# Layer 1 as seven half-size products, q read in PSUM, and sums kept in idle gather rows

## The chip, the cores and the metric

The kernel runs on one core of a Trainium2 chip. The metric is device time in microseconds (us) of one execution; lower is better. All data is 32-bit floating point, and a TensorE product in that type is recorded as two passes.

## The reference

x is (32, 512, 1024): 32 batches, each a matrix of 512 rows (channels) by 1024 columns (nodes). adj is 512 x 512. For every batch:

```python
q, k = wq . x, wk . x                         # 1024 numbers each
scores = leaky_relu(q[None, :] + k[:, None])  # slope 0.01
att = softmax(scores, axis=-1)                # 1024 x 1024
agg = einsum('cn,mn->cm', x, att)
x = layernorm(x + relu(adj @ agg + bm))       # layer 0
W = adj * adj                                 # support and kernel are both adj
x = layernorm(x + W^T @ x + bias)             # layer 1
```

## The kernel before, in words

Layer 0 never forms the 1024 x 1024 attention. Since adj is applied linearly, the kernel first projects x (`project`, L213): for each of 8 column tiles z it makes zrow, a row per node with q, the 512 projected channels and k. With the nodes sorted by q, each softmax row is a combination of a prefix sum and a suffix sum of these rows. So per batch:

- `spread` (L233) puts q along the free axis on all partitions: eight TensorE transposes into a PSUM tile qb, copied to an SBUF tile qs (L241).
- `place` (L256, VectorE) compares qs with the q of one node tile and sums up to that tile's ranks; `send` (L268, GpSimd) scatters the rows of zrow to DRAM in rank order. `count` (L292, ScalarE) counts with a Sign how many q lie above -k, and `top` (L286) takes the largest q.
- `fetch` (L317) brings the sorted rows back to SBUF (zs) in nine blocks, `weigh` (L334) makes the weight matrices lw, and `table` (L356) makes the prefix and suffix sums: nine steps, one after the other. A step is a TensorE product into PSUM tile tp, a ScalarE copy to ts (L368), and two small copies of the carry row into zs for the next step: one on GpSimd (L372), one on ScalarE (L374). The table goes to DRAM.
- `share` (L300) makes the indices, `pick` (L381, GpSimd) gathers from the table into g, eight tiles of three rows' length each (own row, two sums). `shares`, `scale` and `gain` mix the three into u, in place: a ScalarE product (L432) and two VectorE operations (L440) per tile.
- `turn` (L474) transposes u into PSUM and applies the Relu on ScalarE to give y; `join` (L485) adds x and takes the statistics on VectorE; `root` (L454) makes the reciprocal root on GpSimd (L457, L458); `shift` (L461) and `apply` (L467, ScalarE) finish the normalization. Each batch has four row blocks of 128 channels (0 to 3).

Layer 1 (`layer1`, L494) multiplies y by w1, which is adj * adj plus the identity, so that the residual is part of the product. A batch takes 4 x 2 output tiles of 128x512, each a sum of 4 products: 32 products. `stats1` (L515) adds the bias while reading PSUM, and takes the statistics of v.

The batches overlap, three or four at a time. The order on each engine is written out by hand (`tc.manual_schedule()`); each engine runs its own queue strictly in the order of the program, and the build puts semaphore waits where data or buffers require them. `slot(s)` (L659) is one step of the pipeline, for s from 1 to 29:

- TensorE projects batch new = s + 2 tile by tile (z from 0 to 7); in the later half it also runs the table steps of mid = s + 1 and the turns of batch s, and old = s - 1 is normalized and stored.
- then come the spread of new, the last table step of mid and layer 1 of s, with place, count, send, pick and fetch issued among the products.

`begin`, `opening` and `end` fill and drain the pipeline. PSUM has two pools: `ps_mm` with three tiles of two banks for projections, turns, spread and layer 1, and `ps_t` with one for the table steps.

Of the kernel before, what the change touches and what calls it, by code (L numbers as in the profile page):

```python
# [8 lines left out]
F32 = mybir.dt.float32  # L9
# [14 lines left out]
def gat_gcn_resnorm_kernel(  # L24
# [37 lines left out]

    nc = tc.nc
# [19 lines left out]
    gpool = ctx.enter_context(tc.tile_pool(name="gpool", bufs=1))  # L83
# [107 lines left out]

    w1 = adj_sb
    nc.vector.tensor_tensor(w1, adj_sb, adj_sb, ALU.mult)
    for ct in range(CT):
        nc.vector.tensor_tensor(
            w1[:, ct, ct * P : (ct + 1) * P], w1[:, ct, ct * P : (ct + 1) * P], ident, ALU.add
        )

# [5 lines left out]
    gs = {}  # L204
# [28 lines left out]
    def spread(b, copy=nc.scalar.copy):  # L233

        qb = ps_mm.tile([P, N], F32, name=f"qb_{b}", tag="mm")
        for nt in range(NT):
            nc.tensor.transpose(  # L237
                qb[:, nt * P : (nt + 1) * P], zrow[:, nt, 0:1].to_broadcast([P, P]), ident
            )
        qs = junk.tile([P, N], F32, name=f"qs_{b}", tag="qs")  # L240
        copy(qs, qb)  # L241
# [114 lines left out]
    def table(b, step, by=nc.gpsimd):  # L356

        lt, td = tabs[b][0], tds[b].rearrange("(s w u) c -> s w u c", w=2, u=3)
        tp = ps_t.tile([P, 2, H], F32, name=f"tp_{b}_{step}", tag="t")
# [21 lines left out]
    def pick(b, mt):  # L381

        idx = info[b][0]
        if mt == 0:
            gs[b] = gpool.tile([P, NT, 3 * ZW], F32, name=f"g_{b}", tag="g")
        nc.gpsimd.indirect_dma_start(  # L386
            out=gs[b][:, mt, :],
# [7 lines left out]
    def own(b, k0=0, k1=NT):  # L395

        idx, ac, kc, tl = info[b]
        if k0 == 0:
            g = gs.pop(b).rearrange("p k (u c) -> p k u c", u=3)
            ra = small.tile([P, NT, 3], F32, name=f"ra_{b}", tag="ra")  # L400
            mixes[b] = (g, ra)
# [92 lines left out]
    def layer1(b, mt, h, cts=range(CT), op=None):  # L494

        yt = ys[b]
        if op is not None:
            ops[b, mt] = op
        elif (b, mt) not in ops:
            ops[b, mt] = ps_mm.tile([P, N], F32, name=f"o1_{b}_{mt}", tag="mm")  # L500
        for ct in cts:
            nc.tensor.matmul(  # L502
                ops[b, mt][:, h * H : (h + 1) * H],
                w1[:, ct, mt * P : (mt + 1) * P],
                yt[ct][:, h * H : (h + 1) * H],
                start=(ct == 0),
                stop=(ct == CT - 1),
            )

    def layer1g(b, mts, ct):  # L510
        for mt in mts:
            for h in range(NH):
                layer1(b, mt, h, (ct,))

    def stats1(b, mt):  # L515
        t = vpool.tile([P, N], F32, name=f"v_{b}_{mt}", tag="v")
        nc.vector.tensor_tensor(t, ops.pop((b, mt)), bias_bc, ALU.add)  # L517
        stats((1, b, mt), t)
        vs[b, mt] = t
# [4 lines left out]
    def last(b, mt):  # L524

        t = vpool.tile([P, N], F32, name=f"v_{b}_{mt}", tag="v")
        st = small.tile([P, NH, 6], F32, name=f"st_1_{b}_{mt}", tag="st")
        mv = small.tile([P, 2], F32, name=f"mv_1_{b}_{mt}", tag="mv")
        halves = [slice(h * H, (h + 1) * H) for h in range(NH)]
        ops_last = (  # L530
            ps_t.tile([P, N], F32, name="last_0", tag="t"),
            ps_mm.tile([P, N], F32, name="last_1", tag="mm"),
        )
        for h in range(NH):
            layer1(b, mt, h, op=ops_last[h])
        for h, some in enumerate(halves):
            op = ops_last[h]
            nc.vector.tensor_tensor(t[:, some], op[:, some], bias_bc[:, some], ALU.add)
            nc.vector.bn_stats(st[:, h, :], t[:, some])
            if h == 0:  # L540
                shift(1, b, mt - 1)
                apply(1, b, mt - 1)
                store(b, mt - 1)
        nc.vector.bn_aggr(mv, st)
        due[1, b, mt] = [t, mv]
        root(1, b, mt)
        shift(1, b, mt)
        t, mv, rs, nb = due.pop((1, b, mt))
        nc.scalar.activation(t[:, halves[0]], t[:, halves[0]], AF.Identity, bias=nb, scale=rs)
        nc.vector.tensor_scalar(  # L550
            t[:, halves[1]], t[:, halves[1]], rs, nb, ALU.mult, ALU.add
        )
        for some in halves:
            nc.sync.dma_start(out=out[b, mt * P : (mt + 1) * P, some], in_=t[:, some])

    def begin():
# [5 lines left out]
        spread(0)  # L562
# [16 lines left out]
        spread(1)  # L579
        for z in range(NT):  # L580
# [14 lines left out]
            if z == NT // 2 - 1:  # L595
                for mt in range(NT // 2):
                    pick(0, mt)
# [7 lines left out]
            if z == NT - 3:  # L605
                table(1, 0)
                for mt in range(NT // 2, NT):
# [5 lines left out]
        spread(2)  # L613

    def opening():

        shares(0, 0, NT // 2)
        for k in range(NT // 2):
            scale(0, [k])
            gain(0, [k])  # L620
            if k % 2:
                table(1, 3 + k // 2)
        share(1)
        shares(0, NT // 2, NT)
        for k in range(NT // 2, NT):
            scale(0, [k])
            gain(0, [k])
            if k % 2:
                table(1, 3 + k // 2)
# [9 lines left out]
        for mt in range(NT):  # L639
            pick(1, mt)  # L640
        for nt in range(NT):
            order(2, nt)
            count(2, nt)
        top(2)
        fetch(2)
        for ct in range(CT):
            layer1g(0, range(CT - 1), ct)
# [203 lines left out]
```

## Time and profile before

| what | us |
|---|---|
| median of 3 runs (2403.43 to 2408.95) | 2404.76 |
| the profiled execution, its own time | 2408.18 |
| its span, from first to last instruction | 2406.5 |
| TensorE busy (PE) | 2304.5 |
| VectorE busy (DVE) | 1671.5 |
| ScalarE busy (ACT) | 1440.2 |
| GpSimd busy (POOL) | 1019.1 |

The mean granted TensorE clock was 0.98 of full speed. In the profile, PE is TensorE's matmul and PEld its weight load, DVE is VectorE, ACT ScalarE, POOL GpSimd and SP the queue that issues most transfers. L502 means line 502 of the kernel. A group's line reads: line, engine, operation, output<-inputs, shape, count, then busy time and the mean duration of one in ns, then the idle time of the engine just before and what ended it. A line of a timeline reads: start, duration, engine, line, operation, and in brackets the idle time before it. Matmuls are pipelined, so a group's mean duration is longer than the distance from start to start.

### The profile page before, as it was taken

Reading aid. Unit: us, or ns where it says so; the run is one execution under the profiler, and the core shown is the slowest. Engines: PE = TensorE matmul, PEld = TensorE weight load, DVE = VectorE, ACT = ScalarE, POOL = GpSimd, SP = SyncE. Lnnn points to the kernel's source line nnn. Section 1 sums busy time; section 2 is a strip of 40 time slices with the busy share of each in tenths; the row PEclk is TensorE's granted clock in tenths of the full one; section 3 lists DMA queues with packets and bytes.
Section 4 is the critical chain, followed back from the end, with each engine's and each line's share of the span. In section 5 each row is a group of like instructions: output and inputs, shape, how many; then the busy total and the mean of one; then the engine's idle time right before and its main releaser. Section 6 shows DMA issues by size and latency. Waiting matters only on the chain.

```text
span 2406.5 us, 30937 instructions
## 1 busy us (share of the span) xinstructions
PE 2304.5 (96%) x9744; PEld 1450.5 (60%) x9744; DVE 1671.5 (69%) x3485; ACT 1440.2 (60%) x2213; POOL 1019.1 (42%) x1289
## 2 busy tenths in 40 slices
PE   8778999999999999999999999999999999999876
PEld 7545665666665666656566666566666556666433
DVE  3266777767777676777776777767677777677745
ACT  2465656765665775655676655667565566666642
POOL 1333444434444433444533444543444453344431
PEclk9988999999999999999999999999999999999987
DMA  6556777667776767776767777676777676777651
GB/s 241 166 182 219 252 237 250 215 222 250 250 254 230 234 208 241 256 250 231 249 206 232 248 259 242 234 233 212 244 254 253 229 246 206 235 248 252 204 198 48
DMA packets 176836, 548.68 MB, mean 228 GB/s; under 512 B 26304, under 2 KB 26304, under 8 KB 176672
## 3 DMA queue, kind: packets, MB, share of 16 engines
q1 hardware_dynamic: 117600, 276.65, 39.1%
q0 software_dynamic: 57344, 269.52, 29.5%
q8 instruction: 78, 1.28, 0.2%
q14 instruction: 86, 0.70, 0.1%
q10 hardware_dynamic: 1728, 0.53, 0.1%
HBM read 338.17 MB, written 208.43 MB: 227 GB/s over the span
## 4 chain that ended last, share of the span: by engine, by line
PE 78%; DMA 5%; DVE 5%; ACT 4%; issue 4%; POOL 4%; SPq 0%; POOLq 0%; ACTq 0%; DVEq 0%
PE zp L221 32%; PE o L502 30%; PE tp L363 11%; PE op L478 3%; DVE g L440 3%; DMA g<-td,idx 3%; POOL zs L372 2%; ACT y L482 1%; PE qb L237 1%; ACT w L344 1%; DMA zs<-td 1%; ACT ts L368 1%; DVE st L449 1%; DMA td<-zrow,ranki 1%; POOL td L271 1%
## 5 line engine op out<-in xcount | busy, mean ns | idle before, releaser
L221 PE MATMUL zp<-wmT,x 128*128 128x257 f32 x4096 | 968.3, 388 | 3.0 <-ACT zrow L229 3.0
L502 PE MATMUL o<-y,adj_sb 128*128 128x512 f32 x2032 | 891.1, 596 | 6.5 <-ACT y L470 3.6
L221 PEld LDWEIGHTS zp<-wmT,x 128*128 128x128 f32 x4096 | 764.3, 191 | 202.1 <-issue 92.5
L502 PEld LDWEIGHTS o<-y,adj_sb 128*128 128x128 f32 x2032 | 382.1, 191 | 478.6 <-issue 464.2
L372 POOL COPY zs<-ts 1x513 f32<-1x513 f32 x254 | 203.1, 800 | 671.8 <-ACT ts L368 671.8
L440 DVE SCALAR_TENSOR_TENSOR g<-g,ra 128x512 f32<-128x512 f32 x512 | 370.5, 750 | 36.7 <-ACT g L432 27.6
L271 POOL DMA_INDIRECT td<-zrow,ranki x256 | 283.1, 1106 | 194.7 <-DVE ranki L266 124.9
L363 PE MATMUL tp<-zs,lw 128*64 128x257 f32 x2304 | 324.1, 400 | 40.4 <-POOL zs L372 29.7
L229 ACT COPY zrow<-zp 128x514 f32<-128x514 f32 x256 | 148.7, 581 | 327.4 <-PE zp L221 314.5
L262 DVE SCALAR_TENSOR_TENSOR lt<-qs,zrow,first 128x1024 int8<-128x1024 f32 x256 | 326.8, 1277 | 3.7 <-ACT qs L241 2.2
L386 POOL DMA_INDIRECT g<-td,idx x256 | 267.1, 1043 | 89.2 <-issue 78.9
L296 ACT ACTIVATE sg<-qs,kc 128x1024 int8<-128x1024 f32 x256 | 294.1, 1149 | 7.0
L489 DVE TENSOR_TENSOR y<-y,x 128x1024 f32<-128x1024 f32 x128 | 156.8, 1225 | 155.8 <-ACT y L482 154.1
L363 PEld LDWEIGHTS tp<-zs,lw 128*64 128x64 f32 x2304 | 149.4, 138 | 182.6 <-POOL zs L372 70.6
L457 POOL TENSOR_SCALAR rs<-mv 128x1 f32<-128x1 f32 x256 | 78.7, 307 | 400.5 <-ACT v L470 295.0
L368 ACT COPY ts<-tp 128x514 f32<-128x514 f32 x288 | 168.7, 586 | 109.9 <-PE tp L363 106.6
L408 ACT ACTIVATE ac<-s 128x4 f32<-128x4 f32 x64 | 13.3, 208 | 331.6 <-DVE s L407 331.6
L432 ACT ACTIVATE g<-g,ra 128x512 f32<-128x512 f32 x256 | 167.4, 713 | 57.8 <-DVE ra L419 57.7
L458 POOL TENSOR_TENSOR rs<-rs,mhalf 128x1 f32<-128x1 f32 x256 | 186.5, 728 | 21.3
L464 DVE SCALAR_TENSOR_TENSOR nb<-mv,rs 128x1 f32<-128x1 f32 x256 | 39.9, 159 | 217.9 <-POOL rs L458 217.9
L517 DVE TENSOR_TENSOR v<-o,bias_bc 128x1024 f32<-128x1024 f32 x127 | 154.6, 1218 | 31.7 <-PE o L502 31.5
L470 ACT ACTIVATE v<-v,nb,rs 128x1024 f32<-128x1024 f32 x126 | 154.8, 1231 | 33.0 <-DVE nb L464 33.0
(77 smaller groups left out, 1623.7 us busy)
## 6 DMA issues: line engine op xcount, KB each, us to landing
x<-in_x_dram SPq DMA_DIRECT2D x128, 512.0 KB, 3.7
out_dram<-v SPq DMA_DIRECT2D x127, 512.0 KB, 5.5
td<-ts SPq DMA_DIRECT2D x512, 120.5 KB, 2.2
zs<-td SPq DMA_DIRECT2D x64, 602.3 KB, 6.9
zs<-td SPq DMA_DIRECT2D x64, 240.9 KB, 3.5
zs<-td SPq DMA_DIRECT2D x96, 120.5 KB, 3.5
td<-ts SPq DMA_DIRECT2D x64, 96.4 KB, 2.9
td<-zs SPq DMA_DIRECT2D x8, 514.0 KB, 9.5
```

Of the source, the lines that this page charges most:

```text
L221: nc.tensor.matmul(zp[:, h, 0:CE], xb[ct][:, nt * P : (nt + 1) * P], wmT[:, ct, h * CE : (h + 1) * CE], start=(ct == 0), stop=(ct == CT - 1),)
L262: nc.vector.scalar_tensor_tensor(lt, qs, zrow[:, nt, 0:1], first[:, o : o + N], ALU.subtract, ALU.is_lt, accum_out=rank[:, nt : nt + 1],)
L271: sc = nc.gpsimd.indirect_dma_start(out=td[:, :], out_offset=bass.IndirectOffsetOnAxis(ap=ranki[:, nt : nt + 1], axis=0), in_=zrow[:, nt, ...
L296: nc.scalar.activation(sg, qs, AF.Sign, bias=kc[:, nt : nt + 1], accum_out=sgn[:, nt : nt + 1])
L363: nc.tensor.matmul(tp[i * G : (i + 1) * G, h, 0:CE], lt[:, i, j, :], zs[:, j, h * CE : (h + 1) * CE], start=True, stop=True,)
L368: nc.scalar.copy(ts.rearrange("p (h c) -> p h c", h=2), tp[:, :, 0:CE])
L372: by.tensor_copy(zs[0:1, to, 1:ZW], ts[0:1, 1:ZW])
L386: nc.gpsimd.indirect_dma_start(out=gs[b][:, mt, :], out_offset=None, in_=tds[b].rearrange("(s u) c -> s (u c)", u=3), in_offset=bass.Indir ...
L432: nc.scalar.activation(u, u, AF.Copy, scale=ra[:, k, 1:2])
L440: nc.vector.scalar_tensor_tensor(u, g[:, k, i, 1 : C + 1], ra[:, k, i : i + 1], u, ALU.mult, ALU.add)
L458: nc.gpsimd.tensor_tensor(rs, rs, mhalf, ALU.pow)
L502: nc.tensor.matmul(ops[b, mt][:, h * H : (h + 1) * H], w1[:, ct, mt * P : (mt + 1) * P], yt[ct][:, h * H : (h + 1) * H], start=(ct == 0), ...
```

## The change

1. `layer1` splits w1 and y into quarters (256 channels by 256, and 256 by 512) and forms seven products of quarters in place of eight, after Strassen's scheme in Winograd's form. It needs four sums of w1's quarters, S1 to S4, made once, and four sums of y's quarters per batch, T1 to T4. A product is two output tiles of 128x512, each a sum of two: 28 products of 128x512 a batch. The results lie in a PSUM tile per product; `read` adds them into v on VectorE, 18 operations of 128x512 a batch.
2. `sums` makes T1 on VectorE and T2 to T4 on GpSimd, into parts of the gather tile (now one constant tile, `rows`) whose rows 5 to 7 are not yet gathered for the next batch; pick 5, 6 and 7 wait until the products have read them.
3. In the slots `spread` leaves q in PSUM (in `ps_t`), and place, count and top read it there.
4. The slot is ordered anew: turns and joins run from z = 4 in place of 3, the old batch's v is normalized in pairs (0 and 1 on VectorE, 2 and 3 on ScalarE), and `phase` holds the new order of spread, layer 1 and exchange.

```diff
+    lo, hi = slice(0, H), slice(H, N)
+    nc.vector.tensor_tensor(bias_bc[:, hi], bias_bc[:, hi], bias_bc[:, lo], ALU.subtract)
...
+    rows = const.tile([P, NT, 3 * ZW], F32, name="rows")
+    room = {
+        ("T1", 0): (5, 2), ("T2", 0): (5, 0), ("T2", 1): (5, 1),
+        ("T1", 1): (6, 0), ("T3", 1): (6, 2), ("T3", 0): (6, 1),
+        ("T4", 0): (7, 0), ("T4", 1): (7, 2),
+    }
...
-    def spread(b, copy=nc.scalar.copy):
-        qb = ps_mm.tile([P, N], F32, name=f"qb_{b}", tag="mm")
+    def spread(b, copy=False):
+        pool, tag = (ps_mm, "mm") if copy else (ps_t, "t")
+        qs = pool.tile([P, N], F32, name=f"qb_{b}", tag=tag)
...
-        qs = junk.tile([P, N], F32, name=f"qs_{b}", tag="qs")
-        copy(qs, qb)
+        if copy:
+            qb, qs = qs, vpool.tile([P, N], F32, name=f"qs_{b}", tag="v")
+            nc.scalar.copy(qs, qb)
...
+    def sums(b, *some):
...
+            of, less = {
+                "T1": (y1[:, hi], y1[:, lo]), "T2": (y2[:, hi], t1),
+                "T3": (y2[:, hi], y1[:, hi]), "T4": (y2[:, lo], t2),
+            }[name]
+            (nc.vector if name == "T1" else nc.gpsimd).tensor_tensor(t, of, less, ALU.subtract)
...
+        for w, y in (
+            ("A11", "Y11"), ("S1", "T1"), ("S2", "T2"), ("S3", "T3"),
+            ("S4", "Y22"), ("A22", "T4"), ("A12", "Y21"),
+        ):
+            for m in range(2):
+                mul.append(lambda w=w, y=y, m=m: make(w, y, m))
+        for m in range(2):
+            u, v = m, 2 + m
+            for name, what in (
+                ("c1", (u, lo, "A11", m)),
+                ("c5", (v, hi, "S1", m)),
+                ("u2", (u, hi, "S2", m, u, lo)),
+                ("u3", (v, lo, "S3", m, u, hi)),
+                ("u4", (u, hi, None, m, v, hi)),
+                ("12", (u, hi, "S4", m, u, hi)),
+                ("22", (v, hi, None, m, v, lo)),
+                ("21", (v, lo, "A22", m, v, lo)),
+                ("11", (u, lo, "A12", m, u, lo)),
+            ):
...
+    def phase(s, mid, new, step=None):
+        mul, get, reads = layer1(s)
+        def rank(*some):
+            for nt in some:
+                if step is not None:
+                    place(new, nt)
+                    count(new, nt)
+                if nt < 3:
+                    send(new, nt)
+        if step is not None:
+            table(mid, step, pool=ps_mm)
+        mul[0]()
+        mul[1]()
+        sums(s, ("T2", 1), ("T3", 1), ("T4", 1))
+        rank(0, 1, 2)
+        mul[2]()
+        mul[3]()
+        get["c1", 0]()
+        rank(3)
+        get["c1", 1]()
+        rank(4, 5)
+        for mt in range(5):
+            pick(mid, mt)
+        reads("c5")
+        mul[4]()
+        mul[5]()
+        pick(mid, 5)
+        rank(6)
+        get["u2", 0]()
+        rank(7)
+        get["u2", 1]()
+        send(new, 3)
+        send(new, 4)
+        mul[6]()
+        mul[7]()
+        pick(mid, 6)
+        for nt in range(5, NT):
+            send(new, nt)
+        reads("u3", "u4")
+        mul[8]()
+        mul[9]()
+        reads("12", "22")
+        mul[10]()
+        mul[11]()
+        pick(mid, 7)
+        fetch(new)
+        reads("21")
+        mul[12]()
+        mul[13]()
+        shares(mid, 0, NT // 2)
+        scale(mid, range(NT // 2))
+        reads("11")
+        gain(mid, range(NT // 2))
+        if step is not None:
+            top(new)
...
     def slot(s):
...
         for z in range(NT):
-            step, ot = 2 * (z - tz), z - oz
+            step, ot = 2 * (z - tz), z - tz
+            if z == NT - 1:
+                turn(s, CT - 1)
+                sums(s, ("T1", 0), ("T1", 1))
+                join(s, CT - 1)
+                root(0, s, CT - 1)
+                sums(s, ("T2", 0), ("T3", 0), ("T4", 0))
             project(new, z, 0)
...
             if step >= 0:
-                table(mid, step + 1)
+                table(mid, step + 1, pool=ps_mm if z == NT - 1 else ps_t)
...
+            if ot == 2:
+                for mt in (2, 3):
+                    shift(1, old, mt)
+                    apply(1, old, mt)
+                    store(old, mt)
...
-        spread(new, nc.vector.tensor_copy)
-        layer1(s, 0, 0, range(0, CT // 2))
-        table(mid, NB - 1)
...
+        spread(new)
+        shift(0, s, CT - 1)
+        apply(0, s, CT - 1)
+        phase(s, mid, new, NB - 1)
```

## The prediction

> **What bounds the kernel now.** The page first: TensorE is busy almost all the time, and the two costliest groups are its own.
>
> ```profile
> span 2406.5 us, 30937 instructions
> PE 2304.5 (96%) x9744; PEld 1450.5 (60%) x9744; DVE 1671.5 (69%) x3485; ACT 1440.2 (60%) x2213; POOL 1019.1 (42%) x1289
> L502 PE MATMUL o<-y,adj_sb 128*128 128x512 f32 x2032 | 891.1, 596 | 6.5 <-ACT y L470 3.6
> ```
>
> Layer 1 (L502) is 891 us. Next, TensorE's timeline of one slot, from the spread of q (L237):
>
> ```profile
> 1030.16 1.09 PE L237 MATMUL qb<-ident,zrow 128*128 128x128 f32 x8
> 1031.09 1.88 PE L502 MATMUL o<-y,adj_sb 128*128 128x512 f32 x4
> 1032.90 1.09 PE L363 MATMUL tp<-zs,lw 128*64 128x257 f32 x8
> 1033.92 26.02 PE L502 MATMUL o<-y,adj_sb 128*128 128x512 f32 x60
> 1059.77 14.08 PE L221 MATMUL zp<-wmT,x 128*128 128x257 f32 x64
> ```
>
> The columns are start and duration. A pass of 128x512 costs (1059.77 - 1033.92)/60 = 0.431 us. The spreads of slots 1 and 29 start at 246.92 and 2241.55, so a slot takes 71.24 us, some 0.3 of it idle. The 29 slots are most of the span. So what counts is whether TensorE stays fed; which waits would end last is read from the other engines' timelines. VectorE (place) and ScalarE (count) work on one q at the same time:
>
> ```profile
> 1034.03 1.28 DVE L262 SCALAR_TENSOR_TENSOR lt<-qs,zrow,first 128x1024 int8<-128x1024 f32 x1
> 1035.42 1.27 DVE L262 SCALAR_TENSOR_TENSOR lt<-qs,zrow,first 128x1024 int8<-128x1024 f32 x1
> 1034.52 1.15 ACT L296 ACTIVATE sg<-qs,kc 128x1024 int8<-128x1024 f32 x1
> 1035.79 1.15 ACT L296 ACTIVATE sg<-qs,kc 128x1024 int8<-128x1024 f32 x1
> ```
>
> A place every 1.39 us and a count every 1.27, side by side. The tail of a row block goes from engine to engine:
>
> ```profile
> 1095.87 1.11 ACT L482 ACTIVATE y<-op,bm_sb 128x1024 f32<-128x1024 f32 x1 [0.28 <-PE op L478]
> 1097.01 1.23 DVE L489 TENSOR_TENSOR y<-y,x 128x1024 f32<-128x1024 f32 x1 [1.66 <-ACT y L482]
> 1098.27 1.29 DVE L449 BATCH_NORM_STATS2 st<-y 128x6 f32<-128x512 f32 x2
> 1099.59 0.21 DVE L451 BATCH_NORM_AGGREGATE mv<-st 128x2 f32<-128x12 f32 x1
> 1100.54 0.60 POOL L372 COPY zs<-ts 1x513 f32<-1x513 f32 x1 [1.84 <-ACT ts L368]
> 1101.13 0.21 POOL L457 TENSOR_SCALAR rs<-mv 128x1 f32<-128x1 f32 x1
> 1101.42 0.57 POOL L458 TENSOR_TENSOR rs<-rs,mhalf 128x1 f32<-128x1 f32 x1
> ```
>
> Here GpSimd's carry copy (L372), which the next table step on TensorE needs, stands ahead of the root (L457, L458) of the last row block: nothing on TensorE waits for that root at once.
>
> **The change, part by part.** Below, every time is in us, U is the start of the last table step ahead of the spread (step 7), and order and waits are those of the built programs.
>
> *Removed from TensorE.* 56 passes for 64: 8 x 0.431 = 3.45 a slot, on the path. That leaves 71.24 - 0.3 - 3.45 = 67.5 of TensorE work. The three layer-1 passes outside the slots save 10 more; I let sums and waits there eat that, net 0 (between -10 and +20).
>
> *Reads and sums on VectorE.* Out go four additions of 128x1024 (1.22, pitch 1.26) and the copy of qb (1.23); in come 18 of 128x512 (0.69 by L538, pitch 0.72: 13.0), two T1 (1.4) and two applies moved from ScalarE (0.81 each by L472): +10.6, VectorE 51.9 to about 62 of a slot. That fits only while it seldom waits.
>
> *q read in PSUM.* In the changed program each place waits for the count before it on ScalarE, and each count for its place; before, there is no such wait. Place 1.28, handing over 0.05, count 1.25 with its accumulator read, 0.05: 2.63 a pair. The first count also stands behind the copy of table step 8. (A count from PSUM is not in the trace; ScalarE's copy of qb took 1.01 and its Sign from SBUF 1.15, so 0 to 1.1 less in all.) Queued behind these waits on VectorE are the reads that free PSUM for TensorE. VectorE's queue from U: first count ends 5.6, place 3 ends 12.1, both c1 12.9, place 5 17.4, both c5 18.9, place 7 22.9, second u2 23.6, ten reads to 30.8, shares 1.55 to 32.4, two reads to 33.8, eight gain operations of 0.74 to 39.7, top 1.4 to 41.1, shares 42.7, a wait for scale 0.8, eight more gains 49.4, first weights (lw) 49.9. TensorE without waits would stand at the first table step at U + 43.5: spread to 2.0, carry 0.5, table 1.0, products 24.2, four projections 13.9, half of one 1.84. So **6.4** is lost: 1.5 where S4 needs S1's buffer (c5), 1.3 where A22 needs S2's (u2), 3.5 at the table step. Bounds 4 and 8. On the old order places and counts would overlap and the chain would lose nearly 10 of its length, leaving TensorE ahead by little or nothing.
>
> The Trainium skill's "PSUM — Partial Sum Buffer", section "PSUM bank collisions raise a hardware error", says that two engines must not be in one bank and quadrant together, reads against reads included; it speaks against reading q there from two engines. By that rule the waits can't be spared; without it the overlap of the rows above would go on and this 6.4 would be about 0.
>
> *Sums on GpSimd.* T2, T3, T4 of row 0 stand in GpSimd's queue behind the root of row block 3 and ahead of step 6's carry copy, for which TensorE's step 7 waits. Turn and join run one z later, and the old slot's v 2 and 3 are applied on ScalarE ahead of row block 3's Relu. From the start O of row block 2's transposes: Relu ends O + 2.5, add, statistics and aggregate 5.3; ScalarE does copies to 5.9, y 1 to 7.15, v 2 to 8.4, v 3 to 9.6, the Relu to 10.7; add, statistics, aggregate 13.5; root 14.5; three sums of length d; copy 0.65. Step 7 starts at O + 15.2 + 3d where TensorE would be at O + 9.5 (0.96 + 1.84 + 1.02 + 0.96 + 1.84 + 1.02 + 1.84): a stall of 5.7 + 3d. The price d is not in the trace. GpSimd's copy of 513 elements took 0.60 undisturbed, 0.80 in the mean, 1.19 at 1083.79 beside VectorE's work, with one operand; a sum has two. I take 1.0, so **8.7**, with 7.5 (d = 0.6) to 10.5 (d = 1.6) as bounds. If ScalarE were free at once, it would still be 1.2 + 3d. Then the carry of step 7, with only the spread beside it: 0.5; before, four passes (1.8) covered it.
>
> The Trainium skill's "GPSIMD Engine Reference", section "3.1 Elementwise — side-by-side cycle accounting", has 2293 ns for VectorE and 4497 for GpSimd on a sum of 2048 elements; the trace's 128x2048 product on VectorE (L193) took 2293 too. By the page's figures an estimate for 512 is 1.24, and the forecast would be some 20 us higher.
>
> *The clock.* After a long gap the trace shows TensorE slow:
>
> ```profile
> 121.19 2.25 PE L363 MATMUL tp<-zs,lw 128*64 128x257 f32 x8 [9.61 <-DVE lw L349]
> 123.37 5.59 PE L221 MATMUL zp<-wmT,x 128*128 128x257 f32 x16
> 89.16 3.38 PE L221 MATMUL zp<-wmT,x 128*128 128x257 f32 x8
> ```
>
> After 9.61 idle the table took 2.25 for 1.09; the third line, after 2.69 idle, 3.38 for 2.01. So each slot's tail stall costs some 2 behind it, and the 3.5 stall perhaps 1.5; but part falls into waits. I take **2.2**, bounds 0 and 4.4.
>
> *Moved at no charge.* send, pick, fetch: the last send is issued at about U + 25, before 27 behind the spread, and the weights come at U + 49. GpSimd's and SP's issues (some 1 us each) lie beside TensorE's products; if that cover went, ScalarE's weights would come late at the same table step. New v stores on SP stand ahead of table 6's writes, which only the picks need.
>
> *Sum.* 67.5 + 0.5 + 6.4 + 8.7 + 2.2 = 85.3 a slot, +14.1 on 71.24. Times 29: +408 on the profiled execution's 2408.18 (span 2406.5; the runs' median is 2404.76, 0.1% less): **2815 us**.
>
> **Rivals.** *The tail alone.* VectorE's backlog hides behind the tail stall or in shorter operations, and the sums are as short as the copies: 67.5 + 0.5 + 8.7 + 1.5 = 78.2, +7.0 x 29 = 203: 2611. For it: VectorE idles some 20 us of a slot now. Against it: that idle time lies late in the slot, the backlog early.
>
> *Faster.* GpSimd's sums land before TensorE needs the carry, and every wait hides: 32 x 3.45 = 110, so 2298. It decides by one mechanism: the Relu-to-carry chain of row block 3. At its very shortest the stall is 1.2 + 3d = 3.0 with d = 0.6, and 0.5 for the spread's carry, against 3.45 + 0.3 saved: 0.3 a slot, 2400. Only with a sum under 0.5 does it leave a visible gain, and with the ScalarE queue as built there is none.
>
> *No change*: the same chain at d of 0.6 with nothing else late, about 2404.
>
> That products would not shrink is no rival: the built program has 28 products of the same shape for 32.
>
> **How the numbers follow.** The forecast 0.72 (its own range, by the bounds 67.5 + 0.5 + 4 + 7.5 + 0 = 79.5 and 67.5 + 0.5 + 8 + 10.5 + 4.4 = 90.9, is 2648 to 2978, its upper end needing every bound at once), the tail alone 0.20, faster 0.05, no change 0.03. The range 2600 to 2900 takes in the tail alone and leaves out the top corner and the faster cases. Beyond 0.2% (what a measurement of this kernel can tell from no change): faster 0.05, within 0.03, slower 0.92.
>
> **What would show it.** In the profile after: place and count alternating at about 2.6 a pair; in TensorE's timeline a gap of 7 to 10 ahead of step 7, put down to GpSimd's carry copy, with the 128x512 sums just before that copy; a gap ahead of the first table step put down to VectorE's lw or gain; granted clock under 0.95; TensorE busy near 80%. I am wrong if TensorE has no gap over 3 in a slot, or the sums take less than 0.5.

## The result, and the profile after

The changed kernel takes 2767.35 us (median of four runs, 2762.05 to 2772.4) against 2405.57 for the kernel before on the same chip: 1.150 times as long, with a 95% interval of 1.1476 to 1.1528. The forecast was 2815, with 2600 to 2900 as its range. The page of the profiled execution:

```profile
span 2764.6 us, 31176 instructions
PE 2274.5 (82%) x9488; PEld 1422.4 (51%) x9488; DVE 1959.3 (71%) x4035; ACT 1356.4 (49%) x2150; POOL 1191.8 (43%) x1481
L394 PE MATMUL tp<-zs,lw 128*64 128x257 f32 x2304 | 361.5, 431 | 343.3 <-POOL zs L403 292.0
```

TensorE does fewer instructions (9488 for 9744) and is busy 30 us less, but its share has fallen from 96% to 82%. The third line says where it stands idle: 343.3 us ahead of table steps, 292.0 of them until GpSimd has copied the carry (L403). TensorE's timeline over one slot shows them one by one. The columns are start, duration, engine, line, operation, tiles, shape, count, and in brackets the idle time just before and what ended it:

```profile
1240.09 2.01 PE L250 MATMUL zp<-wmT,x 128*128 128x257 f32 x8
1250.47 1.98 PE L394 MATMUL tp<-zs,lw 128*64 128x257 f32 x8 [8.37 <-POOL zs L403]
1252.38 1.97 PE L267 MATMUL qb<-ident,zrow 128*128 128x128 f32 x8
1254.28 1.36 PE L394 MATMUL tp<-zs,lw 128*64 128x257 f32 x8
...
1270.48 3.70 PE L552 MATMUL oS<-y,ws 128*128 128x512 f32 x8 [0.90 <-DVE v L562]
1275.03 3.70 PE L552 MATMUL oA<-rows,adj_sb 128*128 128x512 f32 x8 [0.85 <-DVE v L562]
...
1299.40 1.28 PE L394 MATMUL tp<-zs,lw 128*64 128x257 f32 x8 [1.58 <-DVE lw L380]
```

There is the tail's gap ahead of step 7, then a table step and a spread at half speed (1.98 and 1.97 for the 1.09 of before; the granted clock was 0.50 from 1250.4 to 1254.3), short waits at S4 and A22 (the products of these quarters, each of which needs a PSUM tile that VectorE has not finished reading), and one at the first table step for lw, the first weights. GpSimd's timeline says what stood ahead of the copy that ended the 8.37 us:

```profile
1246.52 1.09 POOL L535 TENSOR_TENSOR rows<-y,rows 128x512 f32<-128x512 f32 x1
1247.57 1.26 POOL L535 TENSOR_TENSOR rows<-y,y 128x512 f32<-128x512 f32 x1
1248.79 1.09 POOL L535 TENSOR_TENSOR rows<-y,rows 128x512 f32<-128x512 f32 x1
1249.82 0.60 POOL L403 COPY zs<-ts 1x513 f32<-1x513 f32 x1
```

The three sums of row 0 took 3.30 us and the copy came next. The next fence shows VectorE (place) and ScalarE (count) reading q in PSUM, in the slot before:

```profile
1177.18 1.28 DVE L293 SCALAR_TENSOR_TENSOR lt<-qb,zrow,first 128x1024 int8<-128x1024 f32 x1 [1.08 <-ACT sg L327]
1179.75 1.28 DVE L293 SCALAR_TENSOR_TENSOR lt<-qb,zrow,first 128x1024 int8<-128x1024 f32 x1 [0.47 <-ACT sg L327]
1178.51 1.11 ACT L327 ACTIVATE sg<-qb,kc 128x1024 int8<-128x1024 f32 x1 [1.36 <-DVE lt L293]
1181.08 1.11 ACT L327 ACTIVATE sg<-qb,kc 128x1024 int8<-128x1024 f32 x1 [1.36 <-DVE lt L293]
```

Place and count take turns, a pair every 2.57 us, where the kernel before ran a place every 1.39 beside a count every 1.27.

Summed up: spreads 4 and 32 start at 260.75 and 2571.23, so 28 slots take 82.52 us each, 11.28 more than the 71.24 of before. Up to the fourth spread it is 13.8 us later (260.75 against 246.92), and one slot's loss lies in that. From the last spread to the end it is 193.4 us against 164.9. So 358 us = 29 x 11.28 + 2.5 + 28.5.

### The profile page after: what moved, and what is told of

Read it like the earlier page. It is cut to its first block, busy times and chain, and to the rows that moved or that the text cites. A ratio compares the mean times of both kernels' runs of the same rounds, so it can differ in the third digit from the quotient of the medians.

```text
span 2764.6 us, 31176 instructions
## 1 busy us (share of the span) xinstructions
PE 2274.5 (82%) x9488; PEld 1422.4 (51%) x9488; DVE 1959.3 (71%) x4035; ACT 1356.4 (49%) x2150; POOL 1191.8 (43%) x1481
## 5 line engine op out<-in xcount | busy, mean ns | idle before, releaser
L394 PE MATMUL tp<-zs,lw 128*64 128x257 f32 x2304 | 361.5, 431 | 343.3 <-POOL zs L403 292.0
L293 DVE SCALAR_TENSOR_TENSOR lt<-qb,zrow,first 128x1024 int8<-128x1024 f32 x232 | 297.6, 1283 | 341.6 <-PE qb L267 192.0
L327 ACT ACTIVATE sg<-qb,kc 128x1024 int8<-128x1024 f32 x232 | 258.7, 1115 | 277.2 <-DVE lt L293 277.2
L469 DVE SCALAR_TENSOR_TENSOR rows<-rows,ra 128x512 f32<-128x512 f32 x512 | 368.6, 751 | 34.3 <-ACT rows L461 25.3
L403 POOL COPY zs<-ts 1x513 f32<-1x513 f32 x254 | 193.1, 760 | 334.4 <-ACT ts L399 334.1
L415 POOL DMA_INDIRECT rows<-td,idx x256 | 271.2, 1059 | 87.5 <-issue 67.8
L552 PE MATMUL oA<-y,adj_sb 128*128 128x512 f32 x512 | 243.8, 618 | 26.6 <-DVE v L562 19.1
L552 PE MATMUL oS<-rows,ws 128*128 128x512 f32 x512 | 229.0, 598 | 4.4 <-DVE rows L535 2.8
L461 ACT ACTIVATE rows<-rows,ra 128x512 f32<-128x512 f32 x256 | 167.2, 713 | 57.5 <-DVE ra L448 55.8
L507 PE MATMUL op<-ident,rows 128*128 128x128 f32 x1024 | 152.6, 292 | 35.0 <-DVE rows L469 35.0
L552 PEld LDWEIGHTS oA<-y,adj_sb 128*128 128x128 f32 x512 | 96.6, 195 | 153.0 <-issue 113.1
L535 POOL TENSOR_TENSOR rows<-y,rows 128x512 f32<-128x512 f32 x128 | 152.0, 1188 | 42.1 <-ACT y L499 38.5
```

Source lines behind the costliest of these rows:

```text
L293: nc.vector.scalar_tensor_tensor(lt, qs, zrow[:, nt, 0:1], first[:, o : o + N], ALU.subtract, ALU.is_lt, accum_out=rank[:, nt : nt + 1],)
L327: nc.scalar.activation(sg, qs, AF.Sign, bias=kc[:, nt : nt + 1], accum_out=sgn[:, nt : nt + 1])
L394: nc.tensor.matmul(tp[i * G : (i + 1) * G, h, 0:CE], lt[:, i, j, :], zs[:, j, h * CE : (h + 1) * CE], start=True, stop=True,)
L403: by.tensor_copy(zs[0:1, to, 1:ZW], ts[0:1, 1:ZW])
L415: nc.gpsimd.indirect_dma_start(out=rows[:, mt, :], out_offset=None, in_=tds[b].rearrange("(s u) c -> s (u c)", u=3), in_offset=bass.Indire ...
L461: nc.scalar.activation(u, u, AF.Copy, scale=ra[:, k, 1:2])
```

## The experiments

The theory on test: the slot is longer since sums, the root and the applies stand in the queues of GpSimd and ScalarE ahead of what TensorE's table steps need, and since place and count take turns on q ("the turns" below; turn 0 and the like are the function `turn`). The rivals are given with each run. "Slot" is the mean over 28 slots from the starts of the spreads, "end" the time from the last spread; the ratio is to the kernel before on the same chip.

| kernel | median us | ratio, 95% interval | slot | end |
|---|---|---|---|---|
| the change | 2767.35 | 1.1476 to 1.1528 | 82.52 | 193.4 |
| e1 sums of row 0 behind step 7's carry | 2674.54 | 1.1104 to 1.1141 | 79.33 | 193.7 |
| e2 = e1, root behind step 6's carry | 2589.52 | 1.0747 to 1.0783 | 76.34 | 194.9 |
| e5 = e2, v 2 and 3 applied on VectorE | 2559.95 | 1.0627 to 1.0662 | 75.41 | 193.6 |
| e3 = the change, places ahead of counts | 2702.61 | 1.1224 to 1.1262 | 80.29 | 192.8 |
| e4 = before, q read in PSUM | 2664.56 | 1.1057 to 1.1094 | 80.23 | 170.4 |
| e7 = e5, places ahead of counts | 2557.88 | 1.0620 to 1.0655 | 75.19 | 193.3 |
| e8 = e7, y 2 applied behind step 7 | 2586.85 | 1.0741 to 1.0777 | 76.26 | 193.6 |
| e9 = e8, slot put in another order | 2438.75 | 1.0114 to 1.0148 | 71.19 | 193.7 |
| e10 = e9, GpSimd's queue shorter | 2422.81 | 1.0040 to 1.0087 | 70.63 | 198.8 |
| e11 = e10, end rewritten | 2409.00 | 1.0003 to 1.0023 | 70.59 | 181.6 |
| e12 = e11, T3 on VectorE | 2376.20 | 0.9856 to 0.9893 | 69.73 | 175.0 |
| e13 = the change, pairs in the end | 2759.59 | 1.1449 to 1.1487 | 82.39 | 184.5 |

**e1: the sums by themselves.** In `slot`, one line is moved from ahead of the last projection to just ahead of `spread(new)`, behind the carry copy of step 7:

```diff
                 root(0, s, CT - 1)
-                sums(s, ("T2", 0), ("T3", 0), ("T4", 0))
...
+        sums(s, ("T2", 0), ("T3", 0), ("T4", 0))
         spread(new)
```

> The changed kernel with one edit: T2, T3 and T4 of row 0 stand on GpSimd behind the carry copy of table step 7 in place of ahead of step 6's. Theory (the tail stall is GpSimd's order): the gap ahead of step 7, 8.4 us a slot, loses the three sums (3 x 1.2), so some 4.8 stay, and the time falls by 29 x 3.6 = 104 to about 2660 us. Rival (VectorE's load bounds the slot, and GpSimd's wait only covers it): the gap moves to the first table step (lw) and less than 30 us is won.

Measured: 93 us less, near the theory's 104. On TensorE's timeline the wait ahead of step 7 is shorter by 3.6, about the length of three sums:

```profile
1208.37 1.98 PE L394 MATMUL tp<-zs,lw 128*64 128x257 f32 x8 [4.80 <-POOL zs L403]
```

So the sums are 3.2 us of the slot's 11.3. The step is still at half speed after a 4.80 us gap.

**e2: the root of row block 3.** It too is moved, behind the table step that comes next:

```diff
                 join(s, CT - 1)
-                root(0, s, CT - 1)
...
             table(mid, step)
+            if z == NT - 1:
+                root(0, s, CT - 1)
```

> As the one before, and row block 3's root also stands behind step 6's carry copy. Theory: what is left ahead of step 7 is ScalarE's queue (v 2, v 3, the Relu of block 3 and y 2 ahead of the copy of step 6), 3.5 to 4 us, so about 1 us a slot less than the one before, and some more clock: 2610 to 2640 us. Rival (the gap is the root's and the sums' alone): the gap goes below 1 us and the time to about 2520.

Measured: another 85 us less, more than the theory expected and less than the rival. The gap is 2.65 to 2.92 us, and in 18 of 29 slots the step behind it runs at full speed:

```profile
1173.17 1.09 PE L394 MATMUL tp<-zs,lw 128*64 128x257 f32 x8 [2.65 <-POOL zs L403]
1174.19 1.09 PE L267 MATMUL qb<-ident,zrow 128*128 128x128 f32 x8
```

Two lines moved in GpSimd's queue thus give back 178 of the 362 us.

**e5: the two v applies off ScalarE.** The edit is `apply(1, old, mt, by=nc.vector)` for v 2 and v 3.

> As the one before, and v 2 and v 3 are applied on VectorE in place of ScalarE, so that the Relu of row block 3 is not behind them. Theory: the gap ahead of step 7 falls to 1 to 2 us, and with it the half clock behind it: 29 x (8.4 - 1.5 + 2) = 260 less than the changed kernel, about 2510 us. Rival (VectorE's load bounds): the 1.7 us more on VectorE show at the first table step, and it is no faster than the one before.

Measured: 2559.95, which is 207 us below the changed kernel where 260 were expected, and 30 below e2. ScalarE's timeline shows why: the apply of y 2 waits for VectorE's small nb, which is now queued behind the two applies and two T1, and step 6's copy is behind that apply.

```profile
1229.37 1.24 ACT L499 ACTIVATE y<-y,nb,rs 128x1024 f32<-128x1024 f32 x1 [1.84 <-DVE nb L493]
```

The work left one queue and its wait came back through another.

**e3: the turns on q.** All counts are issued after all places, so that VectorE never waits for a count:

```diff
         def rank(*some):
             ...
-                    count(new, nt)
...
+        if step is not None:
+            for nt in range(NT):
+                count(new, nt)
         send(new, 3)
```

> The changed kernel with one edit: all eight counts are issued behind the eight places, so that the two engines don't take turns on q's PSUM banks; nothing else is moved. Theory (the turns lengthen VectorE's chain by some 6 us, and 3.3 us of it reach TensorE: 0.8 and 0.85 ahead of products S4 and A22 and 1.6 at the first table step): these gaps close, 29 x 3.3 = 95 less, about 2672 us. Rival (the tail alone): VectorE's backlog is covered by the tail stall, and the time stays within 15 us of 2767.

Measured: 65 us less, two thirds of what was expected. The waits at S4 and A22 are gone from the slots, but the one at the first table step has only gone from 1.58 to 1.38, and the tail is as before. What is left there is no backlog of VectorE, since its readings now wait for TensorE's products:

```profile
1162.78 1.29 DVE L562 TENSOR_TENSOR v<-oS,v 128x512 f32<-128x512 f32 x2 [0.70 <-PE oS L552]
1166.21 1.29 DVE L562 TENSOR_TENSOR v<-oA,v 128x512 f32<-128x512 f32 x2 [0.94 <-PE oA L552]
1168.93 0.17 DVE L445 TENSOR_TENSOR ra<-rows,ac 128x12 f32<-128x12 f32 x1 [0.97 <-ACT ac L437]
```

The third line is the first shares: they wait 0.97 us for ScalarE, which now has eight counts ahead of them, and 0.28 in the changed kernel. So 0.7 of the 1.38 may be of e3's own making. In the list of TensorE's waits (total, times, longest) of this kernel:

```profile
PE tp L394 <- POOL zs L403: 290.5, 125, 8.4
PE tp L394 <- DVE lw L380: 44.6, 30, 3.0
```

**e4: the turns on the old order.** The kernel before, with only the copy of qb left out, q in `ps_t`, and the last table step in `ps_mm`:

```diff
-        qs = junk.tile([P, N], F32, name=f"qs_{b}", tag="qs")
-        copy(qs, qb)
+        qs = qb
...
```

> The kernel before with only the reading of q changed as the change does it: spread leaves q in ps_t, place, count and top read it there, the copy is gone, and the last table step's product uses ps_mm. Theory (the two engines take turns on PSUM, and the turns cost what cover the slot lacks): a place comes every 2.6 us in place of 1.39, VectorE's chain to the last gain grows by some 8 us of which some 3 to 5 are taken up by idle time, and the time rises by 29 x 3 to 6: 2490 to 2580 us. Rival (the turns are hidden; only the tail of the change costs): within 15 us of 2405.

Measured: 2664.56, 259 us over the kernel before and above the whole expected range; 9.0 us a slot. The waits:

```profile
PE op L481 <- DVE g L443: 77.5, 73, 3.4
PE op L481 <- ACT zrow L229: 60.5, 29, 2.4
PE o L505 <- DVE v L520: 24.6, 30, 1.7
PE qb L238 <- ACT ts L371: 21.2, 29, 0.7
```

The kernel before had 24.7 for the first and 1.7 for the third, and neither of the others. The growth adds up to 157 us, 5.4 a slot; TensorE's busy time grew by 97 (2304.5 to 2401.2), 3.3 a slot, in slow work behind those gaps, such as a projection of 3.63 us for 2.01. The expectation had counted waits and not the slow work. Not all of it is the turns: the fourth line, 0.7 us a slot, is the spread waiting for the PSUM tile that it now shares with the table steps.

**e7 and e8: both together, and y 2 later.** e7 puts e3's edit on e5:

> The kernel with sums and root late and v 2 and 3 on VectorE, and with places ahead of counts. Theory (the parts add up): places first took 65 us off the changed kernel and takes about the same here, 2490 to 2510 us. Rival (VectorE's load bounds, so a wait closed opens another): less than 30 us.

Measured: 2 us where 65 were expected; the rival had less than 30. The waits at S4 and A22 went (as in e3), and the time came back at the first table step, where the wait for lw grew to 69.5 us in all from e5's 50.3, and in slower work (TensorE is busy 2249.9 us for e5's 2228.5). So a wait in the middle of the slot is worth its length only while nothing later is late by as much. e8 then takes the apply of y 2 out of step 7's way:

> As the one before, and y 2 is normalized on ScalarE behind the copies of table steps 6 and 7. Theory (what is left ahead of step 7 is ScalarE waiting for VectorE's shift of y 2, 1.8 us, ahead of the copy): the gap of 2.2 to 2.5 us closes to under 0.5, 29 x 2 = 58 less, 2430 to 2450 us. Rival (the wait goes to the sums T2, which need y 2): product S2 waits for them and less than 20 us is won.

Measured: 29 us more than e7, where 58 less were expected. The gap at step 7 is gone, but step 8 now waits:

```profile
1171.29 1.98 PE L394 MATMUL tp<-zs,lw 128*64 128x257 f32 x8 [2.63 <-POOL zs L403]
```

GpSimd's timeline of e8 has the root of row block 3 at 1169.81, behind a wait of 3.41 us for VectorE, and step 7's carry copy at 1170.63 behind it. So the waits for carry copies only moved (131.9 us in all for e7's 134.7). What was added comes from VectorE, behind the spread:

```profile
1170.71 3.87 DVE L493 SCALAR_TENSOR_TENSOR nb<-mv,rs 128x1 f32<-128x1 f32 x1 [0.47 <-POOL rs L487]
1173.48 1.08 POOL L535 TENSOR_TENSOR rows<-y,rows 128x512 f32<-128x512 f32 x1
```

One 128x1 operation, 0.17 us on the mean of e7, lasts until GpSimd's third sum is done, in every slot. VectorE's busy time grew by 103 us (2079.3 for 1976.5), and places and the apply of the next y stand behind that operation. On TensorE this shows as 6.6 us more at lw, 8.3 more ahead of projections, and 13 more of slow work. Moving one wait at a time had stopped paying.

**e9: the slot in another order.** On top of e8, six moves at once: turn 0 behind the second half of projection 4; first weights ahead of the last two gains; v's statistics in two halves (z = 4, 5); their roots behind the carry copies; v's applies on VectorE at z = 5, 6; and a pool of six buffers for the small tiles of the norms.

```diff
-                for mt in (0, 1):
-                    stats1(old, mt)
+            if z in (4, 5):
+                for mt in (2 * z - 8, 2 * z - 7):
+                    stats((1, old, mt), vs[old, mt])
...
+            if z in (4, 5):
+                for mt in (2 * z - 8, 2 * z - 7):
+                    root(1, old, mt)
```

> As the one before, and further: the first weights (lw) are made ahead of gain 6 and 7, row block 0's turn comes behind the second half of projection 4, the statistics of v are taken two and two in z = 4 and 5, their roots stand behind carry copies, v is normalized on VectorE in z = 5 and 6, and the small tiles of the normalizations have six buffers in place of three. Theory: the waits for lw (1.4 to 1.6), for step 1's carry (0.5) and the small ones close, TensorE's work of 67.5 us a slot is left with under 1.5 of waits, and the time is 2370 to 2400 us, a little below the kernel before. Rival (VectorE, at some 63 us of work in a slot of 69, can't be kept free of waits): it stays above 2405.

Measured: a slot of 71.19 us, that of the kernel before (71.24), so the same seven products no longer cost more than the eight: the 11.3 us a slot went by order, by the engine that applies v, and by the buffers, all at once. The 3.45 us saved on TensorE are still lost to waits and slow work. Expected were 2370 to 2400 us; the time stays above 2405, as the rival had it. The kernel is still 33 us slower, and 28.8 of these are its end. What is left in the slot:

```profile
PE tp L395 <- POOL zs L404: 84.0, 102, 7.3
PE zp L251 <- ACT zrow L259: 25.7, 27, 2.5
```

**e10: a shorter queue on GpSimd.** The two T4 go to VectorE, and the gathers of rows 6 and 7 are issued ahead of sends 5 to 7.

> The kernel is the reordered slot (e9) with two moves on GpSimd's queue: the two T4 sums go to VectorE behind the readings of c5, and the gathers of rows 6 and 7 are issued ahead of the sends 5 to 7. In e9 every slot has one wait of 2.5 us ahead of a projection (PE zp waits for ScalarE's zrow, 27 times) with a slowed projection (2.93 instead of 2.0) and a slowed table step (1.79 instead of 1.09) behind it; ScalarE's copy stands behind the scaling of rows 4 and 5, that behind the shares of rows 4 to 7, and those behind the gather of row 7, which GpSimd issues at the very end of a queue that is busy without a pause from 1176.9 to 1205.0. Theory (GpSimd's queue is what the remaining wait comes from): the two T4 take 2.5 us out of the queue and three sends of 1.3 us move behind the gather, so the gather of row 7 comes 4 to 6 us earlier (no earlier than A22's product at 1197.5, which frees row 7); the wait and the slow work behind it, 2.5 + 0.9 + 0.7 = 4.1 us, go away: 28 times 3 to 4 us, from 2438.8 to 2325-2355, the slot at 67 to 68.5. Rival (row 7 is held by A22's product and the landing of the gather, 8.9 us after its issue, not by the queue): the gather moves by 1.5 us at most, the wait shrinks from 2.5 to about 1 and 2395-2420 is left; or T4 on VectorE, which stands between the places, pushes the last place and with it the readings, and nothing is won: 2430-2445.

Measured: 16 us less where 84 to 114 were expected (its runs spread from 2410.63 to 2430.76). The wait named did go (0.8 us in the whole run), but the expectation had misread the line above: 2.5 is its longest, and 25.7 over 27 is 0.95 a slot. And lw grew from 3.0 to 18.8 us: ScalarE, which makes the factors for lw, waits 37.4 us in all for the fetched rows (10.1 in e9). The fetch is no later, it starts 36.0 us behind the spread on the mean of 28 slots (36.4 in e9); but TensorE, rid of the other wait, is at its first table step sooner:

```profile
PE tp L395 <- DVE lw L381: 18.8, 19, 2.8
PE zp L251 <- ACT zrow L259: 0.8, 1, 0.8
```

**e13 and e11: the end.** e13 is the changed kernel with one edit in `rest`, the end's copy of layer 1: both half products are issued, then both read; the table steps stay between the halves.

```diff
-            mul[i]()
-            for name in (...)[i // 2]:
-                get[name, i % 2]()
+            mul[2 * p]()
+            mul[2 * p + 1]()
+            reads(*names)
```

> The kernel is the changed kernel with one edit in the end alone, in rest(): both half products of a pair are issued before the first half is read, where the changed kernel reads the first half before it issues the second. Nothing of the 28 slots is touched. In the changed kernel the last spread lies 193.4 us before the end, against 164.9 in the kernel before; its TensorE rows show ten waits of 0.78 us for VectorE's reading ahead of a second half product, 9.70 and 6.24 us ahead of the second half of A11 Y11 of either batch, 2.39 ahead of the very last half product. Theory (the end's cost is the order of half product and reading; it is apart from the slot's): the ten 0.78 go, the second half of A11 Y11 runs inside the 9.70 and the 6.24 (2.0 + 3.8 us of work taken into the wait), and the final readings come up to 2 us later: 10 to 16 us, from 2767.4 to 2751-2757. Rival (VectorE's work in those stretches is what binds, the waits only show it): 0 to 4 us, 2763-2768.

Measured: the end is 8.9 us shorter, between theory and rival. Of the changed kernel's end (first fence) against e13's (second):

```profile
2636.52 1.44 PE L394 MATMUL tp<-zs,lw 128*64 128x257 f32 x8
2647.66 3.59 PE L552 MATMUL oA<-y,adj_sb 128*128 128x512 f32 x4 [9.70 <-DVE v L562]
2666.35 1.98 PE L552 MATMUL oS<-rows,adj_sb 128*128 128x512 f32 x4 [0.78 <-DVE v L562]
```

```profile
2636.41 1.98 PE L552 MATMUL oA<-y,adj_sb 128*128 128x512 f32 x4
2649.39 1.98 PE L394 MATMUL tp<-zs,lw 128*64 128x257 f32 x8 [10.99 <-POOL zs L403]
2663.52 3.60 PE L552 MATMUL oS<-rows,adj_sb 128*128 128x512 f32 x8
```

The waits of 0.78 (nine; the expectation counted ten) went, as the theory has it. The 9.70 did not: the second half of the product now runs ahead of it, and 10.99 us of waiting for the carry copy have taken its place. GpSimd's timeline of e13 says what stood ahead of that copy:

```profile
2645.04 1.47 POOL L535 TENSOR_TENSOR rows<-y,rows 128x512 f32<-128x512 f32 x1 [1.72 <-DVE rows L535]
2646.47 1.26 POOL L535 TENSOR_TENSOR rows<-y,y 128x512 f32<-128x512 f32 x1
2647.70 1.08 POOL L535 TENSOR_TENSOR rows<-y,rows 128x512 f32<-128x512 f32 x1
2648.73 0.60 POOL L403 COPY zs<-ts 1x513 f32<-1x513 f32 x1
```

It is the slot's tail once more: the three sums, here behind VectorE's T1, ahead of a carry. e11 rewrites that too: T1 in VectorE's pauses between the joins, the older statistics behind the first product, the last product in two tiles.

> The kernel is e10 with the end (the last two batches' layer 1) rewritten: both half products of a pair are issued before the first of them is read, T1 is taken in VectorE's pauses between the joins, the second halves of T2 and T3 on VectorE, the statistics of older batches behind the first product, stores as soon as a tile is done, and the last product in two PSUM tiles. In e9 the time from the last spread to the end is 193.7 us against 164.9 in the kernel before; its TensorE rows there show 9.42 us ahead of the second half of A11 Y11, eleven waits of 0.78 ahead of second half products, 6.32 and 4.0 in the last batch and 2.39 ahead of the last product. Theory (the end's cost is the order of half product and reading): waits of 9.4 + 8.6 + some 6 of the 10.3 + 2.4 = 26 us go away: end at 167 to 172, so 22 to 27 us below e10. Rival (VectorE's own work bounds the end, as it is busy without a pause from 2354 to 2384): only the 0.78s of the first of the two batches and the 9.4 go, 10 to 14 us below e10.

Measured: the end falls from 198.8 to 181.6 us (17.2), the median by 13.8, which is the size the rival named. Its reason is another: the 0.78s are gone from both batches, but two table steps now wait for GpSimd's carry copies. The first of these copies waits 0.59 us for ScalarE's copy of the table step, which stands behind an apply of y that waits 1.33 us for VectorE's nb. Ahead of the second stand the older batch's roots, which wait 6.16 us for VectorE's statistics:

```profile
2296.05 1.98 PE L395 MATMUL tp<-zs,lw 128*64 128x257 f32 x8 [4.10 <-POOL zs L404]
2307.92 1.98 PE L395 MATMUL tp<-zs,lw 128*64 128x257 f32 x8 [7.44 <-POOL zs L404]
```

**e12: a version faster than both.** T3 goes to VectorE as well, two counts go behind the first shares' exponential, and the end's statistics go where VectorE waits anyway.

```diff
         get["c1", 1]()
+        sums(s, ("T3", 0), ("T3", 1), by=nc.vector)
         rank(4, 5)
```

> The kernel is the one with the rewritten end (e11) with four moves. In the slot: the two T3 sums go to VectorE behind the readings of c1 (GpSimd keeps only T2), and the last two counts stand behind the exponential of the first shares on ScalarE. In the end: the statistics of the older batch are taken in VectorE's pauses before its last table, the sums of batch 30 are all on VectorE, and those of the last batch's predecessor are spread over the joins. In e11 a slot takes 70.6 us; the waits left in it are 0.77 us ahead of the fifth projection's table step (VectorE's lw waits for ScalarE's w, and that 1.29 us for the fetched first rows, which stand behind GpSimd's sends), 0.83 and 0.51 at steps 7 and 8, and some 0.8 us of slowed steps. Theory (GpSimd's queue bounds what is left): 2.5 us less in the queue takes the 0.77 and half of the slowed steps away, 0.8 to 1.6 us a slot, 22 to 45 in all; in the end the waits of 4.10 and 7.44 us of two table steps for GpSimd's carry copies and 2.83 of the last batch for VectorE's reading go away, 12 to 14 us. From 2409 to 2350-2375, below both kernels. Rival (VectorE, busy without a pause through layer 1, becomes the bound as it takes over 1.3 us of sums a slot): the slot stays at 70.6 or grows, only the end's 12 us come: 2395-2400.

Measured: 2376.20 us, 0.9874 of the kernel before (0.9856 to 0.9893), so 1.3% below it, and 14% below the changed kernel, with the same seven products.

```profile
span 2375.9 us, 31086 instructions
PE 2199.5 (93%) x9488; PEld 1396.5 (59%) x9488; DVE 2064.0 (87%) x4219; ACT 1290.0 (54%) x2096; POOL 1071.6 (45%) x1351
PE tp L395 <- DVE lw L381: 3.4, 3, 2.8
```

VectorE is now busy for 87% of the span and TensorE for 93%. The slot fell by 0.87 us (expected 0.8 to 1.6), the end by 6.6 (expected 12 to 14), so the time is just above the expected 2350 to 2375. One table step in the end still waits 3.77 us for GpSimd.

## Why the prediction was right, and where its sizes were off

Its steps, by its own order:

- *The products.* 9488 TensorE instructions for 9744, as the built programs said; the 3.45 us saved a slot were never the question.
- *The tail, predicted 8.7.* It is 8.37 in the slot shown, put down to GpSimd's carry copy, with the three sums just ahead of it; e1 and e2 show the chain link by link (gap 8.4, then 4.8, then 2.65). Two errors inside the term partly cancel, which is luck: the sums have a pitch of 1.10 us there (1.0 was taken), and the rest of the chain is 5.07, not 5.7. Over the whole run a sum took 1.21 us (233.0 us over 192; 1.188 and 1.265 by its two forms). The Trainium skill's "GPSIMD Engine Reference", section "3.1 Elementwise — side-by-side cycle accounting", led to an estimate of 1.24, which that mean bears out better than the guess from the copies; in the tail the pitch of 1.10 lies between the two.
- *Step 8's carry, predicted 0.5.* It does not show: the spread at half speed covers it. Where the spread of e2 runs at full speed, 0.33 us are there.
- *VectorE's chain, predicted 6.4.* Measured 3.3: 0.90 for 1.5 at S4, 0.85 for 1.3 at A22, 1.58 for 3.5 at lw. This is the term that was mis-sized most. In a slot of e2 whose step 7 runs at full speed, the first table step starts 47.25 behind step 7 (1173.17), and 3.30 of that are waits for VectorE. The rest, TensorE's own work and step 8's carry, takes 43.95, near the predicted 43.5; but the whole, which VectorE's chain sets, is 2.65 shorter than the predicted 49.9. Half a microsecond of this is the pair, 2.57 us and not 2.63 eight times; 1.2 are the ten readings, which come every 0.60 us and not every 0.72. In the changed kernel the slow work behind the tail lengthens both (48.93 and 45.6 in the slot shown), and the waits stay at 3.3. e3 shows that the turns cause S4 and A22, since both go with them, but hardly lw: that wait is left at 1.38 when no backlog is left. The step of the prediction that put the 3.5 at lw on the turns' backlog fell. Without the turns it had the chain lose nearly 10 us; in e3 the stretch from step 7 to the first table step is 46.5 on the mean, for 48.8, since VectorE then waits for the products.
- *VectorE's load, predicted +10.6 a slot.* The prediction's own items add up to +9.7; measured are +8.9 (1699.3 us for 1451.6 over 28 slots). The sum did not use it.
- *The turns.* The Trainium skill's "PSUM — Partial Sum Buffer" ("PSUM bank collisions raise a hardware error") spoke for waits that can't be spared, and the trace has them, 232 places and counts. But what they cost depends on the order: places first saves 2.2 us a slot in the changed kernel (e3) and 0.2 on e5 (e7), while reading q in PSUM costs 9.0 in the old order (e4).
- *The clock, predicted 2.2.* In the slot shown 0.89 + 0.88 + 0.27 behind the tail (1.98, 1.97 and 1.36 for 1.09) and 0.19 at lw: 2.2. On the mean of 28 slots it is 2.5 (TensorE is busy 1959.8 us, 70.0 a slot, for 67.5 of work).
- *Not in the sum*: three waits of 0.50, 0.24 and 0.25 us for carry copies at other steps, 1.0 in all.

So the slot was put 2.8 too long: -0.3 - 0.5 - 3.1 + 1.0 = -2.9. By 29 that is 81 us too many. (The prediction's last addition gives 2816, not 2815.) On the other side, the end and the opening, put at net 0 (up to +20), cost 28.5 + 2.5. These two errors have opposite signs and leave 49 of the 2815 against the profiled execution's 2766.35: the number was nearer than its terms, by luck. The prediction had let sums and waits eat the 10 us saved outside the slots; it had not looked at the order in which `rest` issues a half product and its reading, which e13 prices at 8.9 us, nor at the queues ahead of the end's table steps, which e11 and e12 show.

Of the rivals, "faster" held that only a sum under 0.5 us would leave a gain. A short sum alone would not have done it: e1 takes the sums wholly out of the carry's way and is still 11% slower. e12 shows that it takes another order and another engine for most sums. "The tail alone" (2611) held that VectorE's backlog hides; S4, A22 and lw stand in the slots all the same, and e3 wins 65 us by them. The main mechanism, a carry copy on GpSimd behind the sums and the root, was right, and the signs named for it are there: the pair at 2.57 us, the gap of 8.37, the granted clock of 0.934, TensorE busy for 82%.

## What to carry to other kernels

An operation that is moved onto an engine with time to spare costs nothing only if its place in that engine's queue is behind what the bounding engine waits for: here two lines in another place gave back half of the loss. Look for the small copy or scalar that the chain needs, and for everything that is queued ahead of it on its own engine; then take all the waits of a slot together, since one that is removed alone may come back at the next, as it did in e5, e7 and e8. Ends and openings have their own order, and their own sum.

## What the runs showed of the hardware

- The length of a gap alone did not say whether TensorE slowed down behind it: the table step took 1.98 us after 8.37, 4.80 and, in e8, 2.63 us, but 1.09 after 2.65 in e2 at 1173.17. In e2 itself, another step behind a gap of 2.65 us (at 408.08) took 1.98.
- Reading q from PSUM instead of SBUF left place and count as fast as before (means of 1.283 against 1.277 us and of 1.115 against 1.149): only the turns cost.
- A sum of 128x512 took 1.08 to 1.47 us on GpSimd in the rows shown, and about 0.7 on VectorE (means of 0.708 and 0.704 in e12, by form).
- A 128x1 operation on VectorE with two inputs, started beside GpSimd's sums, ended only with them: 3.87 us in e8 with three sums, 1.04 in the changed kernel with one (at 1246.59), for 0.17 in e7. Why is not shown here.
